# Moving the normalized x and the weight slabs to multiples of 2,048 bytes of a partition

## The chip, the cores and the metric

The kernel runs on one core of a Trainium2 chip. The metric is the device time of one execution in microseconds. Three runs of the kernel before took 344.66, 344.67 and 345.06 us; the median is 344.67 us.

## What is computed

The reference is one block of a gated cross-attention layer, cut here to what matters:

```python
# x: (2, 512, 1024), ctx: (2, 1024, 1024); all float32
x = x + tanh(g_xattn) * matmul(fake_quant(layernorm(x)), fake_quant(ctx))   # per batch
n = layernorm(x)
logits = n @ router_w + router_b            # 16 experts; two chosen per token
y = sum over experts e of gate[:, e] * ((silu(n @ ew1[e] + eb1[e]) * (n @ ew2[e] + eb2[e])) @ ew3[e] + eb3[e])
z = (silu(n @ sw1 + sb1) * (n @ sw2 + sb2)) @ sw3 + sb3                     # shared MLP, 512 hidden columns
x = x + tanh(g_ffn) * (y + z)
```

An expert has 256 hidden columns. With these inputs the tokens choose two experts in all, and the kernel runs those two; branches for other cases are in the program and not taken.

## The kernel before

**Tiling and stages.** The 1,024 tokens are eight tiles X0 to X7 of 128 tokens. The quantized attention is done in bfloat16: `mm` (L233) multiplies the transposed quantized x (`qT`) with the quantized context (`cq`). The MLPs are done in float32r, with every operand split into a high and a low part and three products: high times high, high times low, low times high.

The normalized x, transposed, is what the MLPs read. Its two parts for a batch are XH[b] and XL[b]: 128 partitions by 8 pieces of the row dimension by 512 tokens, 16,384 bytes of a partition each. All hidden layers stream pieces of XH and XL through TensorE as the moving operand, against a 128-column piece of weights as the stationary one:

- `um` (L476): three hidden column blocks of the shared MLP for batch 0, in pieces of 256 tokens. These stand in the start's hand-written order of steps.
- `up_mm` (L327): the rest. One block of batch 1 is done in pieces of 256 tokens (96 matmuls), all others in pieces of 512 tokens (576 matmuls: 192 in the shared MLP, 192 in each expert).

The down projections `down` (L372, L373, L375) and, for the last tile, `down_last` (L360 to L362) stream 512 or 256 columns of the weights, with a 128-token piece of the hidden layer as the stationary operand. There both operands are slabs. `px` (L288) transposes the normalized x, `xh` (L145, L147) and `xl` (L298) write XH and XL from it, and on GpSimd `router_x` (L557) adds both for the router.

**A slab** is one of 22 buffers of 4,096 bytes of a partition in a pool that turns: weights as loaded, their high and low parts, hidden layers, bias rows. Loads go through SyncE's queue.

**Order.** Up to the first blocks of the shared MLP the order is a list of steps written by hand (`START`). After it the order of the code stands, with the router between the hidden layers of the shared MLP, then the shared down projection, then the experts.

**Where tiles lie.** Pools are stacked in the order in which they are opened, and tiles in a pool in the order in which they are made, each at a multiple of 32 bytes. In the program as built, bytes of a partition:

| tiles | before | remainder to 2,048 | after | remainder to 2,048 |
|---|---|---|---|---|
| zero | 18,368 | 1,984 | 16,512 | 128 |
| ones | 20,512 | 32 | 17,536 | 1,152 |
| ident_b | 17,120 | 736 | 18,048 | 1,664 |
| XH0, XL0 | 54,432 and 70,816 | 1,184 | 18,432 and 34,816 | 0 |
| XH1 and XL1, which share their place with qT and cq | 87,200 and 103,584 | 1,184 | 51,200 and 67,584 | 0 |
| the 22 slabs | 138,240 + 4,096 n | 1,024 | 83,968 + 4,096 n | 0 |
| ident | 16,608 | 224 | 174,176 | 96 |
| X0 to X7 | 21,664 + 4,096 n | 1,184 | 177,440 + 4,096 n | 1,312 |
| small tiles of 1,024 or 2,048 bytes | from 120,736 | 928 or 1,952 | from 210,976 | 32 or 1,056 |

Of the kernel before, what the change touches and what calls it, by code (L numbers as in the profile page):

```python
# [9 lines left out]
F32 = mybir.dt.float32  # L10
F32R = mybir.dt.float32r
BF16 = mybir.dt.bfloat16
U8 = mybir.dt.uint8
# [5 lines left out]
P = 128  # L19
D = 1024  # L20
KD = D // P
B = 2
S = 512
TB = S // P
# [7 lines left out]
SC = 2 * INTER // P  # L32
EPS = 1e-5
LOWEST = -3.4028234663852886e38

# the order in which the start's loads and steps are issued, each step as function.arguments
LOADS = "x.1 x.3 c.0 c.1 x.2 c.2 c.3 c.4 c.5 c.6 c.7.0 c.7.1 w.1.1 x.4 b w.1.0 w.0.1 x.5 w.0.0"
# [40 lines left out]
def flamingo_block(  # L78
# [5 lines left out]
    of = out.rearrange("b s d -> (b s) d")  # L84

    const = ctx.enter_context(tc.tile_pool(name="const", bufs=1))
    keep = ctx.enter_context(tc.tile_pool(name="keep", bufs=1))
    small = ctx.enter_context(tc.tile_pool(name="small", bufs=3))
    route = ctx.enter_context(tc.tile_pool(name="route", bufs=1))
    slabs = ctx.enter_context(tc.tile_pool(name="slabs", bufs=22))  # L90
    ps_mm = ctx.enter_context(tc.tile_pool(name="ps_mm", bufs=6, space=bass.MemoryType.PSUM))
    ps_tr = ctx.enter_context(tc.tile_pool(name="ps_tr", bufs=2, space=bass.MemoryType.PSUM))

    def slab(name, dtype, shape=(P, D)):
        return slabs.tile(list(shape), dtype, tag="slab", name=name)

    def bank(name, dtype=F32, shape=(P, 512)):
# [4 lines left out]

# [1 line left out]
    sc_in = const.tile([P, 6], F32, name="sc_in")  # L104
    nc.sync.dma_start(sc_in, scal.partition_broadcast(P))

# [1 line left out]
    X = [keep.tile([P, D], F32, name=f"X{t}") for t in range(NT)]  # L108

    # the engine that starts the DMAs; the paths that are rarely taken use GpSimd's queue  # L110
    dq = [nc.sync]
# [5 lines left out]

# [1 line left out]
    mhalf = const.tile([P, 1], F32, name="mhalf")  # L119
# [4 lines left out]
    make_identity(nc, ident)  # L124
    ident_b = const.tile([P, P], BF16, name="ident_b")
    nc.scalar.copy(ident_b, ident)
# [5 lines left out]
    nc.vector.tensor_scalar(nz, sc_in[:, 0:4], -1.0, None, ALU.mult)  # L132
    # zero points that bf16 holds exactly, less any quantized value, are integers of 0..255
    z8 = const.tile([P, 4], U8, name="z8")
# [20 lines left out]
    H = D // 2  # L155
# [4 lines left out]

# [1 line left out]
    def bn(t, h):  # L162
# [49 lines left out]

# [1 line left out]
    c8_, raws, qT, cq, acc = {}, {}, {}, {}, {}  # L214
# [21 lines left out]

# [1 line left out]
    sq_, md_, xn_, px_ = {}, {}, {}, {}  # L238

    def e(t, h):  # L240
        """The residual and its sum."""
        if h == 0:
            sq_[t] = [small.tile([P, 2], F32, name=f"{n}{t}", tag=n, bufs=4) for n in "sq"]
        xs = X[t][:, half(h)]
        nc.vector.scalar_tensor_tensor(  # L245
            xs, acc[t][h], cx_scale, xs, ALU.mult, ALU.add, accum_out=sq_[t][0][:, h : h + 1]
        )

    def sq(t, h):
        """H^2 times the squared deviations from the mean of half a row, H values."""  # L250
        if h == 0:
            xn_[t] = slab(f"xn{t}", F32)
        s, q = sq_[t]
        nc.scalar.activation(  # L254
            xn_[t][:, half(h)], X[t][:, half(h)], AF.Square,
            bias=s[:, h : h + 1], scale=-float(H), accum_out=q[:, h : h + 1],
        )

    def fm(t, eng):
        """The mean, and what the difference of the halves' means adds to the variance."""  # L260
        s, eng = sq_[t][0], pick(eng)
        d = small.tile([P, 1], F32, name=f"d{t}", tag="d", bufs=4)
        eng.tensor_tensor(d, s[:, 0:1], s[:, 1:2], ALU.subtract)
        eng.tensor_scalar(d, d, d, H / 2.0, ALU.mult, ALU.mult)
        nm = small.tile([P, 1], F32, name=f"nm{t}", tag="nm", bufs=4)
        eng.tensor_scalar(nm, s[:, 0:1], s[:, 1:2], -1.0 / D, ALU.add, ALU.mult)
        md_[t] = nm, d
# [38 lines left out]

# [1 line left out]
    def load_up(name, w1, w2, c):  # L308
# [44 lines left out]
    def down_last(name, t, hid, w3, scale):  # L353
        """A tile in column pieces, each stored as soon as it is done."""
        n = len(hid)
        for lo, w in ((0, 512), (512, 256), (768, 256)):
            cols = slice(lo, lo + w)
            po = bank(f"{name}po{t}_{lo}")[:, :w]
            for c, ((hh, hl), (wh, wl)) in enumerate(zip(hid, w3)):
                nc.tensor.matmul(po, hh[:, ts(t, P)], wh[:, cols], start=c == 0, stop=False)  # L360
                nc.tensor.matmul(po, hh[:, ts(t, P)], wl[:, cols], start=False, stop=False)
                nc.tensor.matmul(po, hl[:, ts(t, P)], wh[:, cols], start=False, stop=c == n - 1)  # L362
            nc.vector.scalar_tensor_tensor(X[t][:, cols], po, scale, X[t][:, cols], ALU.mult, ALU.add)
            dq[0].dma_start(of[ts(t, P), cols], X[t][:, cols])
# [22 lines left out]

    # ================= program =================
    XH, XL = ([keep.tile([P, KD, S], F32R, name=n), None] for n in ("XH0", "XL0"))
    sw1c = lambda c: sw1[:, ts(c, P)].rearrange("(k p) n -> p k n", p=P)  # L390
# [39 lines left out]

# [1 line left out]
    bT = const.tile([P, NB], F32, name="bT")  # L432
# [5 lines left out]

    # TensorE's clock is low until it has been busy for a few microseconds
    zero = const.tile([P, S], BF16, name="zero")  # L440
    nc.vector.memset(zero, 0.0)
# [7 lines left out]

    # biases of the hidden layers, as columns  # L450
    def pb():
# [5 lines left out]

    # shared weights, split: half h of the rows of matrix i, hidden columns c
    def wh(c, i, h, eng):
# [8 lines left out]

    # hidden columns c of tokens lo..lo+255: matrix i, pass p of three
    def um(c, lo, i, p):  # L470
# [38 lines left out]

    # router weights, padded to the columns of a quarter of TensorE, and constants of the router  # L510
    rwf = const.tile([P, KD, QC], F32, name="rwf")
    rb4 = const.tile([P, 1], F32, name="rb4")
    rbi = const.tile([P, E], F32, name="rbi")
    ones = const.tile([P, P], F32, name="ones")
    tie_i = const.tile([P, E], I32, name="tie_i")
# [11 lines left out]
    def stage(b):  # L527
        """The buffers of a batch's attention."""
        qT[b] = keep.tile([P, TB, KD, P], BF16, name=f"qT{b}", tag="xh1")
        cq[b] = keep.tile([P, KD, D], BF16, name=f"cq{b}", tag="xl1")  # L530

    def xx():
        XH[1], XL[1] = (keep.tile([P, KD, S], F32R, name=n, tag=n.lower()) for n in ("XH1", "XL1"))

# [8 lines left out]

# [1 line left out]
    def rt(name, shape=(P, NT, E), dtype=F32):  # L545
# [6 lines left out]
    def router_x(b):  # L552
        """The normalized x, transposed, in one float32 piece."""
        xs = []
        for i in range(4):
            x = slab(f"xf{b}_{i}", F32, (P, 2, S))
            nc.gpsimd.tensor_tensor(  # L557
                x, XH[b][:, ts(i, 2)].bitcast(F32), XL[b][:, ts(i, 2)].bitcast(F32), ALU.add
            )
            xs.append(x)  # L560
        return xs

    # the four quarters of TensorE's columns work at the same time, each on a fourth of the rows of D
    def router_logits(b, lT, xs):
# [19 lines left out]
    def first_max(name, v, n):  # L584
        """One-hot of the first largest of the last n."""
        m = rt(f"{name}m", (P, NT))
# [8 lines left out]

    # of all experts some token chose: 16 - e; of the others: 0
    key = route.tile([P, E], F32, name="key")
# [48 lines left out]
    def next_expert(j):  # L646
        """Of the chosen experts left, the one of lowest index: its index, gates and hidden biases."""
        m = rt(f"m{j}", (P, 1))
# [19 lines left out]

# [1 line left out]
    def expert(j, e, gv, bv, store):  # L670
# [32 lines left out]

    # the rest of the shared MLP's hidden layer, with the router in between
    lT = slab("lT", F32)
# [21 lines left out]

# [1 line left out]
    def attention_exact(b):  # L729
# [64 lines left out]

# [1 line left out]
    n_exp = nc.values_load(n_chosen[0:1, 0:1], min_val=2, max_val=E)  # L796
# [54 lines left out]
```

## Time and profile before

| what | value |
|---|---|
| median of three runs | 344.67 us |
| span of the profiled execution, first to last instruction | 342.9 us |
| TensorE matmuls | 321.7 us busy, 94% of the span |
| TensorE weight loads | 254.5 us, 74% |
| VectorE, ScalarE, GpSimd | 197.0, 95.4 and 79.0 us |
| mean granted TensorE clock | 0.989 |
| matmuls on XH and XL, 128x512 float32r: length of a record | 396 to 397 ns (L327) |
| matmuls on slabs, 128x512 float32r: length of a record | 389 ns (L372, L373, L375) |
| matmuls on cq, 128x512 bfloat16: length of a record | 379 ns (L233) |

The profiled execution's own time is its span of 342.9 us and what lies around it; the runs' median is 1.8 us above that span. The length of a matmul's record holds the way through the array, which overlaps with the next matmul. What a stream of matmuls costs is read from the distance of their starts. A line such as "200.13 44.98 PE e0p L327 x192" in the chain of waits gives the start of a piece, its length, the engine, the tile written, the line of the code, and how many instructions are in it.

### The profile page before, as it was taken

Reading aid. Unit: us, or ns where it says so; the run is one execution under the profiler, and the core shown is the slowest. Engines: PE = TensorE matmul, PEld = TensorE weight load, DVE = VectorE, ACT = ScalarE, POOL = GpSimd, SP = SyncE. Lnnn points to the kernel's source line nnn. Section 1 sums busy time; section 2 is a strip of 40 time slices with the busy share of each in tenths; the row PEclk is TensorE's granted clock in tenths of the full one; section 3 lists DMA queues with packets and bytes.
Section 4 is the critical chain, followed back from the end, with each engine's and each line's share of the span. In section 5 each row is a group of like instructions: output and inputs, shape, how many; then the busy total and the mean of one; then the engine's idle time right before and its main releaser. Section 6 shows DMA issues by size and latency. Waiting matters only on the chain.

```text
span 342.9 us, 4322 instructions
## 1 busy us (share of the span) xinstructions
PE 321.7 (94%) x1673; PEld 254.5 (74%) x1673; DVE 197.0 (57%) x335; ACT 95.4 (28%) x148; POOL 79.0 (23%) x110
## 2 busy tenths in 40 slices
PE   6588899989999999999999999999999999999990
PEld 2244886769998686888888888888888888888870
DVE  3879999879723126736754632494484135834560
ACT  2756877672213135120200002112400012030000
POOL 2795798868600740000000000000000000000000
PEclk9899999999999999999999999999999999999997
DMA  6999920000004033101200091201310400001542
GB/s 207 420 375 391 399 62 0 2 0 2 0 2 123 9 118 122 63 0 59 66 0 0 8 329 33 62 2 32 90 61 2 122 0 2 0 0 50 198 183 74
DMA packets 25892, 31.45 MB, mean 92 GB/s; under 512 B 2492, under 2 KB 19204, under 8 KB 25860
## 3 DMA queue, kind: packets, MB, share of 16 engines
q1 hardware_dynamic: 25860, 31.05, 26.5%
q8 instruction: 17, 0.28, 0.3%
q14 instruction: 15, 0.12, 0.1%
HBM read 26.85 MB, written 4.19 MB: 91 GB/s over the span
## 4 chain that ended last, share of the span: by engine, by line
PE 75%; DVE 8%; POOL 5%; ACT 4%; issue 3%; DMA 2%; SPq 0%; DVEq 0%; POOLq 0%
PE sp L327 16%; PE e1p L327 13%; PE e0p L327 13%; PE sp L476 5%; PE spo L373 4%; PE spo L372 4%; PE spo L375 4%; ACT xn L254 2%; PE e0po L372 2%; PE e0po L373 2%; PE e0po L375 2%; PE e1po L373 2%; PE e1po L372 2%; PE e1po L375 2%; DVE xn L283 2%
## 5 line engine op out<-in xcount | busy, mean ns | idle before, releaser
L233 PE MATMUL at<-cq,qT 128*128 128x512 bf16 x128 | 30.3, 379 | 2.5 <-POOL cq L153 1.5
L557 POOL TENSOR_TENSOR xf<-XH,XL 128x1024 f32<-128x1024 f32 x8 | 19.9, 2497 | 22.4 <-PE sp L327 19.6
L233 PEld LDWEIGHTS <-qT 128*128 128x128 bf16 x128 | 12.1, 98 | 15.5 <-issue 2.9
L378 DVE SCALAR_TENSOR_TENSOR X<-spo,tg,X 128x512 f32<-128x512 f32 x16 | 11.3, 746 | 16.0 <-PE spo L375 16.0
L338 DVE SCALAR_TENSOR_TENSOR ssa<-sp,bT,ssa 128x512 f32<-128x512 f32 (+1 forms) x6 | 4.0, 662 | 26.1 <-PE sp L327 26.1
L337 ACT ACTIVATE e0sa<-e0p,bv 128x512 f32<-128x512 f32 x4 | 2.8, 690 | 49.4 <-PE e0p L327 49.4
L378 DVE SCALAR_TENSOR_TENSOR X<-e0po,gv,X 128x512 f32<-128x512 f32 x16 | 11.3, 747 | 7.3 <-PE e0po L375 7.3
L283 DVE TENSOR_SCALAR xn<-X,nm,d 128x512 f32<-128x512 f32 x16 | 13.8, 891 | 1.4 <-POOL d L279 1.3
L378 DVE SCALAR_TENSOR_TENSOR X<-e1po,gv,X 128x512 f32<-128x512 f32 x14 | 9.9, 747 | 8.2 <-PE e1po L375 8.2
L288 PE MATMUL px<-ident,xn 128*128 128x128 f32 x64 | 9.3, 275 | 3.5 <-DVE xn L283 2.3
L337 ACT ACTIVATE e1sa<-e1p,bv 128x512 f32<-128x512 f32 x4 | 2.8, 690 | 34.9 <-PE e1p L327 34.9
L338 DVE SCALAR_TENSOR_TENSOR e1sa<-e1p,bv,e1sa 128x512 f32<-128x512 f32 x4 | 3.0, 752 | 15.9 <-PE e1p L327 15.9
L254 ACT ACTIVATE xn<-X,s 128x512 f32<-128x512 f32 x16 | 11.4, 716 | 1.9 <-DVE X L245 1.4
L245 DVE SCALAR_TENSOR_TENSOR X<-at,cx_scale,X 128x512 f32<-128x512 f32 x16 | 11.6, 742 | 0.1
L165 DVE BATCH_NORM_STATS2 st<-X 128x6 f32<-128x512 f32 x16 | 10.3, 680 | 2.2 <-DMA X<-in_dram 2.2
L338 DVE SCALAR_TENSOR_TENSOR e0sa<-e0p,bv,e0sa 128x512 f32<-128x512 f32 x4 | 3.0, 751 | 14.6 <-PE e0p L327 14.6
L288 PEld LDWEIGHTS px<-ident,xn 128*128 128x128 f32 x64 | 7.2, 141 | 5.6 <-ACT XH L145 2.6
L298 DVE TENSOR_TENSOR XL<-px,XH 128x512 fp32r<-128x512 f32 x16 | 10.4, 679 | 0.8 <-ACT XH L145 0.8
L386 DVE SCALAR_TENSOR_TENSOR X<-sbias,tg,X 128x1024 f32<-128x1024 f32 x8 | 10.3, 1284 | 0.3
L153 POOL TENSOR_SCALAR cq<-q8c,nz 128x1024 bf16<-128x1024 uint8 (+1 forms) x8 | 10.0, 1250 | 1.0 <-DVE q8c L223 0.6
L208 PE MATMUL pq<-ident_b,qx 128*128 128x128 bf16 x64 | 5.4, 228 | 4.7 <-ACT qx L151 4.4
L386 DVE SCALAR_TENSOR_TENSOR X<-e1bias,gv,X 128x1024 f32<-128x1024 f32 x8 | 9.8, 1280 | 0.0
(402 smaller groups left out, 830.9 us busy)
## 6 DMA issues: line engine op xcount, KB each, us to landing
cr<-in_dram SPq DMA_DIRECT2D x15, 512.0 KB, 9.2
out_dram<-X SPq DMA_DIRECT2D x15, 256.0 KB, 2.4
X<-in_dram SPq DMA_DIRECT2D x7, 512.0 KB, 9.0
X<-in_dram SPq DMA_DIRECT2D x2, 256.0 KB, 4.1
cr<-in_dram SPq DMA_DIRECT2D x2, 256.0 KB, 9.1
sb1r<-in_dram SPq DMA_DIRECT2D x1, 512.0 KB, 9.0
sa1r<-in_dram SPq DMA_DIRECT2D x1, 512.0 KB, 7.2
sb0r<-in_dram SPq DMA_DIRECT2D x1, 512.0 KB, 8.2
```

The lines of the kernel that those rows point to most:

```text
L233: nc.tensor.matmul(acc[t][h], qT[b][:, t % TB, k, :], cq[b][:, k, half(h)], start=(k == 0), stop=(k == KD - 1))
L254: nc.scalar.activation(xn_[t][:, half(h)], X[t][:, half(h)], AF.Square, bias=s[:, h : h + 1], scale=-float(H), accum_out=q[:, h : h + 1],)
L283: nc.vector.tensor_scalar(xn_[t][:, half(h)], X[t][:, half(h)], nm, r, ALU.add, ALU.mult)
L288: nc.tensor.transpose(px_[t, q][:, k, :], xn_[t][:, ts(4 * q + k, P)], ident)
L327: nc.tensor.matmul(p, wx[:, k, :], xx[b][:, k, cols], start=first and k == 0, stop=last and k == KD - 1)
L372: nc.tensor.matmul(po[h], hh[:, ts(t, P)], wh[:, ts(h, 512)], start=first, stop=False)
L373: nc.tensor.matmul(po[h], hh[:, ts(t, P)], wl[:, ts(h, 512)], start=False, stop=False)
L375: nc.tensor.matmul(po[h], hl[:, ts(t, P)], wh[:, ts(h, 512)], start=False, stop=last)
L378: nc.vector.scalar_tensor_tensor(xs, po[h], scale, xs, ALU.mult, ALU.add)
L386: nc.vector.scalar_tensor_tensor(X[t], bb, scale, X[t], ALU.mult, ALU.add)
L476: nc.tensor.matmul(up_[c, lo, i], w[:, k, :], x[0][:, k, lo : lo + 256], start=p == 0 and k == 0, stop=p == 2 and k == KD - 1,)
L557: nc.gpsimd.tensor_tensor(x, XH[b][:, ts(i, 2)].bitcast(F32), XL[b][:, ts(i, 2)].bitcast(F32), ALU.add)
```

## The change

A new pool `wide` is opened first and `slabs` second, ahead of `const`, `keep`, `small` and `route`. Three constants (`zero`, `ones`, `ident_b`) and 128 unused bytes stand in front of `wide` and fill it up to byte 18,432, nine times 2,048. XH, XL, and `qT` and `cq`, which use the same places, are made in `wide`. Everything else follows behind the slabs. Comments are removed as well. The diff without them:

```diff
+PAD = 128
...
+    wide = ctx.enter_context(tc.tile_pool(name="wide", bufs=1))
+    slabs = ctx.enter_context(tc.tile_pool(name="slabs", bufs=22))
     const = ctx.enter_context(tc.tile_pool(name="const", bufs=1))
     keep = ctx.enter_context(tc.tile_pool(name="keep", bufs=1))
     small = ctx.enter_context(tc.tile_pool(name="small", bufs=3))
     route = ctx.enter_context(tc.tile_pool(name="route", bufs=1))
-    slabs = ctx.enter_context(tc.tile_pool(name="slabs", bufs=22))
...
+    zero = wide.tile([P, S], BF16, name="zero")
+    ones = wide.tile([P, P], F32, name="ones")
+    ident_b = wide.tile([P, P], BF16, name="ident_b")
+    wide.tile([P, PAD], U8, name="pad")
...
-    ident_b = const.tile([P, P], BF16, name="ident_b")
...
-    XH, XL = ([keep.tile([P, KD, S], F32R, name=n), None] for n in ("XH0", "XL0"))
+    XH, XL = ([wide.tile([P, KD, S], F32R, name=n), None] for n in ("XH0", "XL0"))
...
-    zero = const.tile([P, S], BF16, name="zero")
...
-    ones = const.tile([P, P], F32, name="ones")
...
-        qT[b] = keep.tile([P, TB, KD, P], BF16, name=f"qT{b}", tag="xh1")
-        cq[b] = keep.tile([P, KD, D], BF16, name=f"cq{b}", tag="xl1")
+        qT[b] = wide.tile([P, TB, KD, P], BF16, name=f"qT{b}", tag="xh1")
+        cq[b] = wide.tile([P, KD, D], BF16, name=f"cq{b}", tag="xl1")
...
-        XH[1], XL[1] = (keep.tile([P, KD, S], F32R, name=n, tag=n.lower()) for n in ("XH1", "XL1"))
+        XH[1], XL[1] = (wide.tile([P, KD, S], F32R, name=n, tag=n.lower()) for n in ("XH1", "XL1"))
```

## The prediction

> **What bounds the kernel now.** I read the page first, then the busy time by stretch, then the chain of waits with its start times, then single instructions in time order. The page says who is full:
>
> ```profile
> PE 321.7 (94%) x1673; PEld 254.5 (74%) x1673; DVE 197.0 (57%) x335; ACT 95.4 (28%) x148; POOL 79.0 (23%) x110
> PE   6588899989999999999999999999999999999990
> ```
>
> TensorE is busy 94% of the span, and from the sixth slice on it hardly stops. Only the first 26 us and the last 9 us belong to others. The stretches show the same over two kinds of work:
>
> ```profile
> 156.57:200.13 43.56, 43.56 (x194) 36.04 (x193) 25.91 (x49) 2.73 (x3) 0.00 (x0) 1.00 0.16 46
> 200.13:245.11 44.98, 44.98 (x193) 36.16 (x193) 21.21 (x21) 8.40 (x11) 0.00 (x0) 1.00 0.27 85
> 266.87:311.85 44.98, 44.98 (x194) 36.16 (x193) 19.93 (x20) 8.40 (x11) 0.00 (x0) 1.00 0.06 20
> ```
>
> The columns are the stretch, its length, then busy time of PE, weight loads, DVE, ACT and POOL, the granted clock, DMA. All three stretches are solid TensorE at the full clock (1.00), with DVE and ACT far from full. The first is the shared down projection (L372 to L375), the other two are the up projections of the experts (L327). Each is 192 matmuls of 128x512 float32r with 192 weight loads (a record or two of the neighbours is counted in). Yet one takes 43.56 us and the others 44.98. The chain of waits gives the same pieces (start, length, what):
>
> ```profile
> 37.56 7.61 PE sp L476 x64
> ...
> 90.30 4.75 PE sp L476 x40
> 95.05 22.64 PE sp L327 x144
> ...
> 134.33 22.02 PE sp L327 x94
> 156.57 0.23 PE spo L372
> ...
> 199.67 0.45 PE spo L375 x2
> 200.13 44.98 PE e0p L327 x192
> ```
>
> So the pitch (start to start) is 44.98/192 = 234.3 ns where the moving operand is XH or XL, and 43.56/192 = 226.9 ns where it is a slab. The x94 piece agrees: 22.02/94 = 234.3. The reader should keep the question: what makes equal matmuls 7.4 ns dearer in one place?
>
> The stationary operand is no answer: in both it is a 128-column piece of a slab, and the weight loads last 188 ns in both. The order of the banks is no answer either. The last tile (L360 to L362) accumulates six times running into one bank, as L327 does into one bank 24 times, and its six 512-wide matmuls take from 330.74 to 332.10 us in the timeline: 227 ns each. What differs is where the moving operand lies. In the program as built XH0 starts at byte 54,432 of a partition, which is 1,184 past a multiple of 2,048 and 32 past a multiple of 64; XL0, XH1 and XL1 follow at multiples of 16,384 and have the same remainder. Slabs start at 138,240 + 4,096 n, which is 1,024 past a multiple of 2,048.
>
> **The change part by part.** It moves tiles to other addresses and does nothing else. The instruction order of all five engines and the semaphores they wait for are the same before and after, the DMA queue of SP and the queue of POOL among them; no instruction is added, removed or moved past another.
>
> *512-wide matmuls on XH and XL (L327).* There are 576: three groups of 192 (the shared MLP's, expert 0's, expert 1's). XH and XL go from remainder 1,184 to 0. I take the slab's pitch as the nearest row for an aligned operand: 192 x (234.3 - 226.9) = 1.42 us a group, 3 x 1.42 = -4.26 us, all on the path.
>
> *256-wide matmuls on XH and XL.* 96 by L327 (95.05 to 106) and 288 by L476. Now: 7.61/64 = 118.9 ns and 4.75/40 = 118.8 ns in L476; in the x144 piece, (22.64 - 48 x 0.2343)/96 = 118.7 ns. The nearest row for 256 columns of a slab is the last tile of the down projection:
>
> ```profile
> 331.87 0.39 PE L362 MATMUL e1po<-e1d1h,e1h1l 128*128 128x512 f32 x1
> 332.10 0.28 PE L360 MATMUL e1po<-e1d0h,e1h0h 128*128 128x256 f32 x1
> ...
> 332.45 0.28 PE L360 MATMUL e1po<-e1d1h,e1h1h 128*128 128x256 f32 x1
> 332.57 0.28 PE L361 MATMUL e1po<-e1d1l,e1h1h 128*128 128x256 f32 x1
> 332.69 0.28 PE L362 MATMUL e1po<-e1d1h,e1h1l 128*128 128x256 f32 x1
> ...
> 333.05 0.28 PE L362 MATMUL e1po<-e1d0h,e1h0l 128*128 128x256 f32 x1
> 333.17 0.28 PE L360 MATMUL e1po<-e1d1h,e1h1h 128*128 128x256 f32 x1
> ```
>
> 332.45 to 333.17 is 0.72 us for six: 120 ns, a little *more* than the 118.8 of today's badly placed XH. So the 256-wide ones may lose: 96 x 1.3 = +0.12 us, and of L476 the 136 that the chain holds (64 at 37.56 us, 8 at 85.62, 24 at 87.00 and 40 at 90.30) x 1.2 = +0.17 us. The other bound is half of the aligned 512-wide pitch, 113.4 ns: -0.51 and -0.73 us. I take 120, the measured row, and keep the other end for the range.
>
> *The slabs*, from remainder 1,024 to 0. Pieces that start at 1,024 (columns 512 to 767) and at 0 (columns 768 to 1,023) both stand in the rows above at 120 ns, so 1,024 is as good as 0: nothing.
>
> *bfloat16 operands* (qT, cq, ident_b, now aligned too). fifteen matmuls of L233 from 49.83 us take 3.41 us in the timeline, the last record 0.38 of it, so (3.41 - 0.38)/14 = 216 ns start to start with cq at remainder 1,184, less than any float32r row, and `zero`, at a multiple of 64, reaches the same 216 once the clock is up: nothing.
>
> *DVE, ACT and POOL on XH and XL.* L298 writes XL in 679 ns; L340, the same subtraction into a slab, takes 0.68 to 0.69 us in the timeline. Alignment shows nothing there, so L145 (585 ns on ACT) and L557 (2.4 us on POOL) stay. Where they didn't, L557 has cover: the second router group ends at 123.44 us and is read at 130.91. TensorE gains 0.36 us before that; 7 us of slack remain.
>
> *X, the small tiles, `ident`* move behind the slabs. X goes from remainder 1,184 to 1,312, `ident` from 224 past a multiple of 256 to 96; both stay 32 past a multiple of 64. Loads of 512 KB land in 9.0 us into X (misplaced) and 9.2 us into slabs (placed), so the DMA does not care. Nothing, with 0.3 us either way for the start, whose chain hops between DVE, ACT and POOL.
>
> *What is late next.* With the up projections shorter, the next weights are wanted sooner. The last split of expert 0's second half (L304) ends at 219.9 us and its matmuls start near 231.8; in expert 1 there is the same gap. 1.4 us a stage eats little of it. DVE is at 21 of 45 us there.
>
> Sum: -4.26 + 0.12 + 0.17 = -3.97 us on the profiled span of 342.9, so 338.9. The median of the runs is 344.67, 1.8 us above the span, which I carry over: 340.7 us.
>
> **A rule that speaks against it.** The Trainium skill, "SBUF — State Buffer", section "Door 1: The DMA port swizzle", in its note on SBUF cachelines, gives lines of 16 bytes and a penalty for crossing to a new one. 54,432 is 3,402 x 16: XH0 already starts on a line, and a contiguous read crosses as many lines as an aligned one. By the rule the move is worth 0 and the time stays 344.7. By the rows it is worth 4 us. I follow the rows, since the rule leaves 43.56 against 44.98 unexplained; a line of 64 bytes would explain it (33 touched for 32), but no row shows its width.
>
> **The rivals.**
>
> *No effect (0.07).* The 7.4 ns belong to something else in which the stages differ, such as XH lying far below the slabs, or 24 accumulations in one bank rather than six. For: only two places are compared. Against: at 512 columns the pitch is 227 for fresh and repeated weights, one bank or two. Time: 344.7.
>
> *Slower by collision (0.05).* Moving stream and weight load would now start at the same remainder, and each matmul of the up stage waits for the other read. For: before, they never shared a remainder. Against: in the down stage both are slabs, so share it already, and run faster. Priced like the difference seen, 576 x 7.4 ns = +4.3: 348.9. It decides from 0.9 ns on each of the 808 matmuls on the path, which makes 0.7 us.
>
> *Larger gain (0.04).* Today every 512-wide float32r read crosses a multiple of 2,048; then none would. If the crossing costs, all fall to L233's 216: 576 x 18.3 + 384 x 10.9 = -14.7 us, 330.0. Against: 227 - 120 = 107 ns for the second 256 columns, [...]hardly more than the full rate that 216 for 512 implies; the 256-wide pieces don't cross and carry the same 13 ns on top.
>
> *Part of the gain (0.04).* Half of the 7.4 ns: about 342.5.
>
> **How the numbers follow.** The forecast holds 0.80. Its own range is 339.2 (256-wide at 113.4) to 341.4 (the start loses 0.7). With the half gain I give 339.0 to 342.5. About 0.2%, 0.7 us, is what a measurement of this kernel tells from no change. Faster by more: 0.80 + 0.04 + 0.04 = 0.88; within: 0.07; slower: 0.05.
>
> **What would show it.** After: 192 matmuls of each expert's up stage in 43.6 us instead of 44.98, their records near 389 instead of 396 ns, the down stage still at 43.56, L476 near 120 ns, L233 still 216. Wrong if the up stage stays at 44.98, or if the down stage moves.

## The result, and the profile after

| | before | after |
|---|---|---|
| median of six runs each | 344.67 us | 340.15 us (339.04 to 342.31) |
| ratio to before, 95% interval | | 0.9865 (0.9844 to 0.9886) |
| span of the profiled execution | 342.9 us | 338.5 us |

The change makes the kernel 1.35% faster. In the kernel after, line numbers are 6 to 9 higher: L327 is now L335, L372 to L375 are L380 to L383, L476 is L483. In the kernels of the experiments, L327 is L330, L335, L336 or L337.

The busy time by stretch after the change, for the same three stretches as before (stretch, length, then busy time of PE, weight loads, DVE, ACT and POOL, granted clock, DMA):

```profile
155.23:198.76 43.53, 43.53 (x193) 36.05 (x193) 25.90 (x49) 2.73 (x3) 0.00 (x0) 1.00 0.16 46
198.76:242.28 43.52, 43.52 (x193) 36.05 (x193) 21.21 (x21) 8.40 (x11) 0.00 (x0) 1.00 0.28 88
264.04:307.56 43.52, 43.52 (x193) 36.05 (x193) 19.93 (x20) 8.40 (x11) 0.00 (x0) 1.00 0.06 20
```

The shared down projection has not moved (43.56 before). The two up stages have come down from 44.98 to the same length. The chain of waits after the change (start, length, what) shows the other pieces:

```profile
37.71 7.68 PE sp L483 x64
...
90.07 4.79 PE sp L483 x40
94.86 22.43 PE sp L335 x144
...
119.14 11.15 PE sp L335 x48
...
133.63 21.38 PE sp L335 x94
...
198.76 43.52 PE e0p L335 x192
...
264.04 43.52 PE e1p L335 x192
```

Two things are to be seen. The 512-wide matmuls went from 234.3 to 43.52/192 = 226.7 ns start to start. The 256-wide ones went *up*, from 118.9 to 7.68/64 = 120.0 ns. Where the 4.4 us of span came from: the experts' up stages 2 x 1.46; the shared MLP's pieces 22.64 - 22.43, 11.44 - 11.15 and 22.02 - 21.38, together 1.14; the start up to 94.86 us 0.19; the rest (0.15) is spread over the down stages and the end.

Numbers and rows came as forecast. The experiments were to show whether the reason was right too, and it was not.

### The profile page after: what moved, and what is told of

It reads as the page before. It is cut to its first block, busy times and chain, and to the rows that moved or that the text cites. A ratio compares the mean times of both kernels' runs of the same rounds, so it can differ in the third digit from the quotient of the medians.

```text
span 338.5 us, 4322 instructions
## 1 busy us (share of the span) xinstructions
PE 318.1 (94%) x1673; PEld 254.7 (75%) x1673; DVE 197.0 (58%) x335; ACT 95.3 (28%) x148; POOL 78.6 (23%) x110
## 4 chain that ended last, share of the span: by engine, by line
PE 75%; DVE 8%; POOL 5%; ACT 4%; issue 3%; DMA 2%; SPq 0%; DVEq 0%; POOLq 0%
PE sp L335 16%; PE e1p L335 13%; PE e0p L335 13%; PE sp L483 5%; PE spo L381 4%; PE spo L380 4%; PE spo L383 4%; ACT xn L262 2%; PE e0po L380 2%; PE e0po L383 2%; PE e0po L381 2%; PE e1po L380 2%; PE e1po L383 2%; PE e1po L381 2%; DMA X<-in_dram 2%
## 5 line engine op out<-in xcount | busy, mean ns | idle before, releaser
L563 POOL TENSOR_TENSOR xf<-XH,XL 128x1024 f32<-128x1024 f32 x8 | 19.9, 2498 | 22.3 <-PE sp L335 19.5
L306 DVE TENSOR_TENSOR XL<-px,XH 128x512 fp32r<-128x512 f32 x16 | 10.4, 678 | 0.8 <-ACT XH L153 0.8
L159 ACT ACTIVATE qx<-q8x,nz 128x1024 bf16<-128x1024 uint8 (+1 forms) x7 | 7.2, 1022 | 9.5 <-DVE q8x L205 9.5
```

Of the source, the lines that this page charges most:

```text
L563: nc.gpsimd.tensor_tensor(x, XH[b][:, ts(i, 2)].bitcast(F32), XL[b][:, ts(i, 2)].bitcast(F32), ALU.add)
```

## The experiments

The theory to test was that of the prediction: a float32r matmul is slow when its moving operand lies off a multiple of 64 bytes. The rivals were a larger multiple, the stationary operand's place, and the absolute place of XH.

**One side misplaced, then the other.** First XH and XL alone are moved 32 bytes off:

```diff
-PAD = 128
+PAD = 96
+    shim = ctx.enter_context(tc.tile_pool(name="shim", bufs=1))
     slabs = ctx.enter_context(tc.tile_pool(name="slabs", bufs=22))
+    shim.tile([P, 32], U8, name="shim32")
```

> The kernel after with XH and XL 32 bytes past a multiple of 64 and the slabs where they are. If the place of the moving operand decides, 192 matmuls of an expert's up stage go from 43.52 back to 44.98 us, the down stage stays at 43.5, the 256-wide pieces go from 120.0 to 118.7 ns, and the time is 340.15 + 576 x 7.4 ns - 232 x 1.3 ns = 344.1 us. If the gain came with the slabs (stationary operand), the up stage stays at 43.5 and the time at 340.2.

Measured: ratio to before 1.000 (0.9985 to 1.0014). The up stage of expert 0 in the chain of waits:

```profile
201.25 44.80 PE e0p L337 x192
```

The gain is gone. This agrees with the theory, but it tells nothing of *why* the place matters. The second kernel keeps XH and XL at multiples of 2,048 and moves the slabs by 32 bytes:

```diff
+    shim = ctx.enter_context(tc.tile_pool(name="shim", bufs=1))
     slabs = ctx.enter_context(tc.tile_pool(name="slabs", bufs=22))
+    shim.tile([P, 32], U8, name="shim32")
```

> The kernel after with XH and XL where they are and the slabs 32 bytes past a multiple of 64. If only the moving operand counts, the up stage stays at 43.5 us (its stationary operand is now misplaced) and 192 matmuls of the shared down projection go from 43.5 to 44.98; 384 x 7.4 ns makes 343.0 us. If the stationary operand counts as well or instead, the up stage is slower too, up to 45 us a group, 347 us in all. X and ident come to multiples of 64 here: px stays at 109 ns start to start if its pitch is set by the weight load, and falls by up to 7 ns if ident as moving operand was slowed by its place.

Measured: ratio 1.0001 (0.9984 to 1.0017). Its busy time by stretch, down stage and expert 0's up stage:

```profile
156.53:200.06 43.53, 43.53 (x193) 36.05 (x193) 25.91 (x49) 2.73 (x3) 0.00 (x0) 1.00 0.16 44
200.06:244.86 44.80, 44.80 (x193) 36.06 (x193) 21.21 (x21) 8.40 (x11) 0.00 (x0) 1.00 0.28 87
```

This is the opposite of the theory on both lines. The down stage, whose moving operand is now 32 bytes off, stays at 43.53. The up stage, whose moving operand lies perfectly, is slow. ident came to a multiple of 64 here and px stayed at 109 ns start to start: in these float32 transposes its place costs nothing.

**Both on multiples of 64.** The kernel before gets two pads of 32 bytes:

```diff
     route = ctx.enter_context(tc.tile_pool(name="route", bufs=1))
+    shim = ctx.enter_context(tc.tile_pool(name="shim", bufs=1))
     slabs = ctx.enter_context(tc.tile_pool(name="slabs", bufs=22))
+    shim.tile([P, 32], U8, name="shim32")
...
+    keep.tile([P, 32], U8, name="pad_x")
     XH, XL = ([keep.tile([P, KD, S], F32R, name=n), None] for n in ("XH0", "XL0"))
```

> The kernel before with 32 unused bytes ahead of XH and 32 ahead of the slabs, nothing else: XH and XL at 1,216 past a multiple of 2,048, slabs at 1,088, both multiples of 64. If 64 bytes are what counts, up stage 43.5 us, 256-wide pieces 120 ns, 340.2 us. If it takes 2,048 (or the new order of the pools), up stage 44.98 and 344.7 us; something between for 128 to 1,024.

Measured: ratio 0.9988 (0.9966 to 1.001). The up stage of expert 0:

```profile
199.71 44.79 PE e0p L330 x192
```

Multiples of 64 on both sides bring nothing that stands clear of the noise. The theory of the prediction had fallen.

**The next theory: the distance.** What the fast cases share is that the moving operand and the weights start on the same remainder. In the down stage both are slabs, so this holds wherever the slabs lie. In the up stage it held only after the change. Call the distance of a matmul the start of the weights' slab minus the start of XH or XL. Before it is 138,240 - 54,432 = 83,808 for slab 0, which is 96 past a multiple of 256; after it is 83,968 - 18,432 = 65,536, which is a multiple of 256. The decisive kernel moves XH, XL, the slabs and all behind them by 32 bytes, so that both operands are misplaced and the distance is kept:

```diff
-PAD = 128
+PAD = 160
```

> The kernel after with everything in and behind the wide pool 32 bytes further: XH, XL and the slabs all 32 bytes past a multiple of 64, so on one remainder. If what counts is that the moving operand and the weights being loaded start on the same remainder, the up stage stays at 43.5 us and the time at 340.2. If what counts is that both lie on a multiple of 64 (or more), the up stage is at 44.8 as with one of them misplaced, and the time is 344.3 us; with the old theory (the moving operand's place alone) it is 344.3 and the down stage is slower too, 347.

Measured: ratio 0.9885 (0.9843 to 0.9927), median 340.41 us. The chain of waits of this kernel:

```profile
199.08 43.52 PE e0p L335 x192
...
264.36 43.52 PE e1p L335 x192
```

With neither operand on a multiple of 64 the whole gain is there. The distance counts, and not the place of either operand.

**Which distances.** Each slab is made 32 bytes longer, so slab n is 32 n bytes further from XH and XL than a multiple of 4,096, and its distance is given as 32 n from here on:

```diff
-        return slabs.tile(list(shape), dtype, tag="slab", name=name)
+        t = slabs.tile([P, D + 8], dtype, tag="slab", name=name)[:, :D]
+        return t if len(shape) == 2 else t.rearrange("p (a b) -> p a b", a=shape[1])
```

> The kernel after with every slab 32 bytes longer, so that slab n starts 32 n past a multiple of 4,096: the distance between the moving operand (XH, XL at 0) and the weights takes 22 values. Each pass of eight matmuls on one weight slab gives a pitch for one distance. If only the same remainder is fast, passes are at 226.7 ns for slabs 0 and the one at the modulus (8 for 256, 16 for 512, none for 1,024 and more) and at 233 to 235 ns for the others; the down stage splits in the same way by the distance between hidden slab and weight slab. If it is the moving operand's own multiple of 64 together with that of the weights, even slabs are fast and odd ones slow. Up to 4 us slower than after.

Measured: 346.33 us in its one run. The timeline of TensorE gives one row for each pass of eight (start, length with the last one's way through the array, operands). Slab sa1h is at distance 608, sa1l at 576, sb1h at 0, sb1l at 32, sa2l at 256, sb2h at 128:

```profile
108.15 2.03 PE L336 MATMUL sp<-XL,sa1h 128*128 128x512 f32 x8
110.02 2.03 PE L336 MATMUL sp<-XH,sa1l 128*128 128x512 f32 x8
111.89 1.99 PE L336 MATMUL sp<-XH,sb1h 128*128 128x512 f32 x8
113.71 1.98 PE L336 MATMUL sp<-XL,sb1h 128*128 128x512 f32 x8
115.53 2.02 PE L336 MATMUL sp<-XH,sb1l 128*128 128x512 f32 x8
...
123.18 1.99 PE L336 MATMUL sp<-XH,sa2l 128*128 128x512 f32 x8
125.00 2.03 PE L336 MATMUL sp<-XH,sb2h 128*128 128x512 f32 x8
126.87 2.02 PE L336 MATMUL sp<-XL,sb2h 128*128 128x512 f32 x8
```

From start to start a pass takes 1.87 us at distance 608 and 576, 1.82 at 0 and at 256, and 1.87 at 128. The single starts in the trace show how a pass at 0 or 256 settles: the first matmuls (three at 0, one at 256) still come at 229 to 232 ns, then all at 226 or 227. Over the whole run, modulo 256, passes settle at 226.7 ns for 0, near 229 for 192, and at 231 to 235 for 32, 64, 96, 128, 160 and 224. Distance 96 is that of the kernel before, and its starts have before's mean of 234.

The down stage was expected to slow down as well, since the distances between its hidden and weight slabs now differ too. This is the only run in which the shared down projection moved, from 43.53 to 44.60 us:

```profile
156.28:200.88 44.60, 44.60 (x194) 36.12 (x193) 25.93 (x49) 2.73 (x3) 0.00 (x0) 1.00 0.16 45
```

The time is 6.2 us above the kernel after, where at most 4 were expected; some 2 us of it are in the down projections of the shared MLP and the experts. One pass at 256 is thin evidence for the modulus, so it was tried cleanly.

**One pad ahead of the slabs, three sizes.** These start from the kernel before; nothing else is changed, and XH stays at 1,184 past a multiple of 2,048. Distances are given less multiples of 2,048.

```diff
     route = ctx.enter_context(tc.tile_pool(name="route", bufs=1))
+    shim = ctx.enter_context(tc.tile_pool(name="shim", bufs=1))
     slabs = ctx.enter_context(tc.tile_pool(name="slabs", bufs=22))
+    shim.tile([P, 160], U8, name="shim")
```

160 bytes, distance 0:

> The kernel before with 160 unused bytes ahead of the slabs and nothing else: XH and XL stay at 1,184 past a multiple of 2,048, the slabs come to 1,184 as well, all of them 32 past a multiple of 64. If the distance from the moving operand to the weights counts, by the staggered run modulo 256, the up stage is at 43.5 us, the 256-wide pieces at 120 ns and the time at 340.2 us: the whole gain of the change by one pad. If places count by themselves, 344.7 us and an up stage of 44.98.

416 bytes, distance 256:

> As the pad of 160 bytes, with 416: the distance is 256. If the modulus is 256, up stage 43.5 us and 340.2 us in all; if it is 512, up stage about 44.8 us and 344 us.

224 bytes, distance 64:

> As the pad of 160 bytes, with 224: the distance is 64. By the staggered run the 512-wide matmuls are at 233.3 ns (up stage 44.8 us) and the 256-wide ones at 114 to 115 ns, faster than with equal remainders (120) and than before (118.8): 344.67 - 576 x 1.0 - 232 x 4 ns = 343.2 us. If what the staggered run showed was an after-effect of the pass ahead, the 256-wide ones stay near 119 and the time is 344.

Measured: 160 bytes 0.9889 (0.9863 to 0.9915), 416 bytes 0.9898 (0.9861 to 0.9935), 224 bytes 0.9953 (0.9937 to 0.9969). The pad of 160 gives the change's up stage; its two stretches, down and up:

```profile
155.65:199.19 43.54, 43.54 (x193) 36.03 (x193) 25.90 (x49) 2.74 (x3) 0.00 (x0) 1.00 0.17 46
199.19:242.71 43.52, 43.52 (x193) 36.04 (x193) 21.22 (x21) 8.41 (x11) 0.00 (x0) 1.00 0.28 88
```

So 160 unused bytes do what the change does, and 416 as well (43.52 us for each expert): the modulus is 256. At distance 64 the up stage is as slow as with the other wrong distances, but the 256-wide passes, in this kernel's timeline of TensorE, are the fastest of all (the last row is the up stage in its chain of waits):

```profile
97.44 1.07 PE L330 MATMUL sp<-XH,sa0l 128*128 128x256 f32 x8
...
101.97 1.07 PE L330 MATMUL sp<-XL,sa0h 128*128 128x256 f32 x8
...
200.19 44.80 PE e0p L330 x192
```

Five passes of eight lie between the first two starts: 4.53/40 = 113.3 ns, against 120.0 at distance 0. That is where its 1.4 us come from: 232 matmuls on the path at 5 ns less are 1.2 us, and 1.0 ns less on 576 is 0.6, in all somewhat more than was measured. The best distance for 512 columns is not the best for 256.

| distance, modulo 256 | kernels | 512 columns, ns | 256 columns, ns |
|---|---|---|---|
| 96 | before | 44.98/192 = 234.3 | 118.8 |
| 32 | XH off by 32; slabs off by 32 | 44.80/192 = 233.3 | 4.73/40 = 118.3 |
| 128 | two pads | 44.79/192 = 233.3 | 4.75/40 = 118.8 |
| 64 | pad of 224 | 44.80/192 = 233.3 | 113.3 |
| 0 | after; all off by 32; pads of 160 and 416 | 43.52/192 = 226.7 | 120.0 |

**One operand alone.** In the kernel after, only XL1 (and cq, in the same place) is moved by 32 bytes, and the slabs by 256, which leaves all other distances at multiples of 256:

```diff
+    shim = ctx.enter_context(tc.tile_pool(name="shim", bufs=1))
     slabs = ctx.enter_context(tc.tile_pool(name="slabs", bufs=22))
+    shim.tile([P, 224], U8, name="shim")
...
         qT[b] = wide.tile([P, TB, KD, P], BF16, name=f"qT{b}", tag="xh1")
+        if b == 0:
+            wide.tile([P, 32], U8, name="pad_xl1")
         cq[b] = wide.tile([P, KD, D], BF16, name=f"cq{b}", tag="xl1")
```

> The kernel after with XL1, and with it cq, 32 bytes further; the slabs are moved by 256, so every other distance stays a multiple of 256. If the distance rules each matmul, a batch 1 pass on XL1 leaves 226.7 ns for about 233 (a third of the 512-wide matmuls of batch 1, 120 of 576: +0.8 us) and the passes on XH and on XL0 stay at 226.7. It is also the first run in which the bfloat16 matmuls have their moving operand (cq) on another remainder than their stationary one (qT): they stay at 216 ns if bfloat16 doesn't care, and go to 220 or more if it does (128 of them, about 0.5 us or more). 340.9 us or so.

Measured: 341.45 us in its one run, against 340.9 expected. TensorE's timeline for expert 0, where the first two rows are the end of batch 0 and the rest is batch 1:

```profile
205.91 1.98 PE L337 MATMUL e0p<-XL,e0b0h 128*128 128x512 f32 x8
207.72 1.98 PE L337 MATMUL e0p<-XH,e0b0l 128*128 128x512 f32 x8
209.53 1.98 PE L337 MATMUL e0p<-XH,e0a0h 128*128 128x512 f32 x8
211.34 2.03 PE L337 MATMUL e0p<-XL,e0a0h 128*128 128x512 f32 x8
213.22 2.01 PE L337 MATMUL e0p<-XH,e0a0l 128*128 128x512 f32 x8
215.06 1.98 PE L337 MATMUL e0p<-XH,e0b0h 128*128 128x512 f32 x8
```

The pass on XL1 takes 213.22 - 211.34 = 1.88 us, with the same weights with which the pass on XH1 just ahead took 1.81. So it is neither the weights nor the batch, but the pair. The pass after it (XH1 again) still takes 1.84: an after-effect that the expectation had not priced. (The matmuls on XL1 are 112 of the 576, not 120.) Expert 0's stage is 43.89 us in all. The bfloat16 matmuls, with cq now 32 bytes off qT, stay at 216 ns.

**A better version.** A float32r matmul at distance 0 costs its columns plus a fixed part: 226.7 - 120.0 = 106.7 ns for 256 columns, which leaves 13.3 ns a matmul. So fewer, wider ones pay. The block of the shared MLP that was done twice over 256 tokens is done once over 512, on top of the kernel after:

```diff
-    for h in range(2):
-        sup(0, 1, 256 * h, 256)
+    sup(0, 1)
```

> The kernel after with the shared MLP's block 0 of batch 1 done once over 512 tokens, not twice over 256: 48 matmuls of 512 for 96 of 256. If a float32r matmul on a well placed operand costs its columns plus a fixed 13 ns, 96 x 120.0 - 48 x 226.7 ns = 0.64 us are saved: 339.5 us. If the second half of XH and XL of batch 1 is not ready when the block starts, TensorE waits and the time is 340.2 or more.

> The merged kernel once more beside the kernel after: 0.64 us faster, 339.5 us, if 48 x 13.3 ns is all that it saves.

> The kernel after once more, for comparison with the merged one on the same chip: 340.2 us.

Measured: ratio to before 0.982 (0.9803 to 0.9837) in its first set. In the second, beside the kernel after on one chip, the merged one had 340.09 us and 0.9871 (0.985 to 0.9892), the kernel after 340.78 us and 0.9904 (0.9886 to 0.9923). The intervals of the second set touch, so the runs there alone don't separate them; the medians differ by 0.69 us. The piece in the chain of waits does, here of the first merged run:

```profile
96.79 21.79 PE sp L335 x96
```

Before the merge this was 144 matmuls in 22.43 us: 0.64 us less, as worked out, and no wait for the second half of XH1.

## Why the prediction was right, and where it was wrong

- *The path.* TensorE is the bound, and a shorter matmul goes into the time in full: right. The median fell by 4.52 us against 3.97 forecast, the profiled span by 4.4. The start was put at +0.17 us and came out at -0.19, although its 256-wide matmuls did lose: a little more than the 0.3 us either way that was allowed for it, and it was not traced further.
- *512-wide matmuls.* The slab's row of the down stage was taken as the price, 1.42 us a group: 1.46 measured in an expert's stage.
- *256-wide matmuls.* The row of the last tile said 120 and a small loss, half of a 512-wide one said 113.4 and a gain. Taking the row was right: 120.0. It fitted for a reason that was not seen: both operands of that row are slabs, at the distance that XH has after the change. The other bound turned up too (113.3), but at distance 64.
- *The reason.* Wrong. The step that failed is "what differs is where the moving operand lies". Slabs were the reference for a well placed operand, but what makes the down stage fast is that both its operands come from slabs, a multiple of 256 apart. Two places were compared that differed in two things, the place and the distance, and I named one. The right price came out because the change puts XH and the slabs on one remainder, in which the prediction saw nothing to gain; that is luck. "The slabs, from remainder 1,024 to 0: nothing" also holds for a reason not given: 1,024 is a multiple of 256, so this move leaves every distance modulo 256, and what closed the distance is XH's and XL's move alone. A move of the slabs by 32 bytes takes the whole gain away (1.0001). If the change had put XH at any multiple of 64, the same reasoning would have forecast 4 us; with two pads XH lies so, and the ratio is 0.9988.
- *The collision rival* named the right variable, the shared remainder, with the wrong sign, and the profile's argument against it (the down stage shares it and is the faster one) was the clue that I used only to dismiss it.
- *The rule of 16-byte lines* says that XH's place by itself costs nothing. The kernels with everything off by 32 bytes, and the pad of 160, agree: an operand 32 past a multiple of 64 runs at 226.7 ns. The line of 64 bytes that I offered in its place is refuted.
- *The larger gain* did not come: no float32r matmul of 512 columns settled below 226 ns in any run. Its price is too high as well, since it counts 384 matmuls of 256 columns where the path holds 232: -13.1 us and 331.6, not -14.7 and 330.0.
- *The rest.* L306 writes XL in 678 ns (679 before), GpSimd's sums take 2,498 (2,497; the prediction's 2.4 us is 2.5), the matmuls on cq 379: nothing, as costed. No new wait came up behind TensorE.

## What to carry to other kernels

When two rows of equal instructions differ, list everything that differs between them, the relation between the operands included, before one cause is priced. For float32r matmuls at 512 columns with a weight load each, let the moving and the stationary tile start a multiple of 256 bytes apart in the partition; one pad ahead of a pool can do it. A row of the same trace may give the right price under the wrong reason, and only kernels that move one side at a time tell.

## What was not expected of the hardware

In float32r the time of a matmul depends on where its two operands lie to each other. The Trainium skill, "TensorE: Matmul & The Clock Gate", section "Step-by-step: what each phase is for", says that loading the next weights takes no read bandwidth from the running matmul; here 512 columns take 226.7 or 233 to 234 ns by the distance of the two operands alone, which speaks against it for this type. That the weight load in flight is the partner, and read bandwidth what they share, is an inference: every matmul here has a load, the loads' busy time hardly differs (36.05 us a stage after, 36.16 before), and no kernel without a load for each matmul was tried. In bfloat16, 32 bytes of distance changed nothing (216 ns). Distances finer than 32 bytes were not tried, and why 256 columns prefer 64 is open.

The granted clock of the start differs between executions, and the time tends to go with it. In the profiled run of the kernel after it was 1.00 from 15 us on; in the merged kernel's first profiled run it was still low up to 45 us (stretch, length, PE, weight loads, DVE, ACT, POOL, granted clock, DMA; first the kernel after, then two rows of the merged one):

```profile
15.00:30.00 15.00, 12.34 (x71) 5.80 (x70) 12.72 (x23) 10.11 (x15) 11.29 (x15) 1.00 1.07 373
...
15.00:30.00 15.00, 13.48 (x71) 6.69 (x71) 12.80 (x21) 10.22 (x15) 11.31 (x14) 0.84 1.04 365
30.00:45.00 15.00, 13.08 (x82) 9.86 (x80) 13.91 (x29) 12.09 (x21) 11.88 (x17) 0.89 1.04 389
```

The merged kernel's first matmuls of L335 start at 96.79 us, those of the kernel after at 94.86. The six runs of the kernel after go the same way in the main, from 339.04 us at a mean clock of 0.991 to 342.31 at 0.980, but the clock is not the whole of it: the kernel with everything off by 32 has 340.48 us at 0.979. A change of 1 us is better read from its stage than from one run.
